# A graph layer and a mixture of experts in one kernel: experts' results wait in DRAM until the edges are done

## The chip, the cores and the metric

The kernel runs on one core of a Trainium2 chip. The metric is device time in microseconds (us) of one launch. Times below are either medians of several runs, or come from one profiled execution, whose trace all views of the profile answer from.

## The reference, cut to what matters

The input is 6250 nodes with 256 features, and 100,000 edges sorted by destination. A layer of graph attention comes first, then a mixture of 8 experts, of which each node uses two. In short form:

```python
xn  = layer_norm(layernorm(x)); h = xn @ W                 # 8 heads of 32
e   = leaky_relu(a_src[src] + a_dst[dst])                  # edges and self loops
agg = segment_softmax_sum(e, h[src], dst)                  # by destination node
o   = layer_norm(agg + xn @ W_res + bias)
x1  = x + o + gelu_tanh(o @ ffn_w1 + ffn_b1) @ ffn_w2 + ffn_b2
p   = softmax(layernorm(x1) @ Wr + br)                     # the two best of 8 experts
out = x1 + sum over the two experts e of
      weight_e * (gelu(ln_e(x1) @ W1[e] + b1[e]) @ W2[e] + b2[e])
```

So every row of `out` is written once (x1) and then has two experts' results added to it.

## The kernel before, in words

All arithmetic is in float32. A first stage (up to about 190 us) normalises the nodes, computes `h` and stores a table `tab_s` of its rows in DRAM.

**The edges.** The edges are handled in 196 steps of four tiles of 128 edges. In a step POOL issues four indirect DMAs that gather rows of `tab_s` by source node (`fetch`, L809), DVE weighs the rows (`weigh`, L847 to L851), and PE adds them up by destination with one-hot matrices (L866, L891). `gs`, the tile of gathered rows, has 4 buffers. The groups of edges run from the last destination to the first, so nodes at the end are finished first.

**Work beside the edges.** While the edges still run, finished nodes go through their own feed-forward network (`node_unit`), choose their experts, and are written to `out` by SP and, with POOL's scatters (`scatter`, L1345), into lists by expert in DRAM (`xs`). As soon as a list has 256 tokens for an expert, a block of experts' work can start (`block_unit`). There are 56 blocks (NB). A block loads 2 MB of weights (`load_weights`, L1388 to L1390) and its 256 tokens (`load_block`, L1396) with SP's queue, transposes the tokens (`turn`, L963 and L970), runs eight parts of the first product (`up`: PE L978, ACT L981 with Gelu) and the second product (`down`: PE L988, into the one PSUM tile `py`). Then, in this order:

- `note` (DVE, L1409 to L1413) copies the destination row numbers from the tokens' tile into the small tile `to` (3 buffers) and works out the weights;
- `finish` (DVE, L1418) adds the bias and moves `py` to `yb`, a tile of 2 x 256 columns with 2 buffers. It frees `py`;
- `weigh_block` (ACT, L1424) multiplies by the weights, 128 rows at a time;
- `give_back` (POOL, L1428) is an indirect DMA that adds 128 rows of `yb` to their rows of `out`. A block needs two. As all of them write `out`, each one waits until the one before has landed.

A buffer of `yb` becomes free when both additions of its block have landed.

**The order.** Nothing is reordered on the chip: each engine, and each queue of DMAs, runs its instructions in the order in which the program issues them. That order is made by a small planner in the kernel. Every operation beside the edges is a `task` with an engine and a cost in us. In each step `run_tasks` issues, oldest first, those tasks whose inputs were issued early enough, until the engine's `room` for this step is used up: `ROOM` while the edges run, `ROOM_AFTER` behind them (`s >= NG + LASTST`, with 196 and 6). One step stands for some 7.7 us of PE's time, and a block is worth about two steps:

```python
g0 = task(lambda: give_back(0, env), "POOL", 2.6, [wb_])
stored.append(task(lambda: give_back(1, env), "POOL", 2.6, [g0]))
```

`stored` holds the tasks after which a buffer of `yb` may be used again: `finish` names the second last of them as an input.

Of the kernel before, what the change touches and what calls it, by code (L numbers as in the profile page):

```python
# [36 lines left out]
F32 = mybir.dt.float32  # L40
I32 = mybir.dt.int32
U32 = mybir.dt.uint32
AF = mybir.ActivationFunctionType
ALU = mybir.AluOpType
# [4 lines left out]
P = 128  # L49
# [12 lines left out]
ROOM = {"PE": 7.5, "DVE": 7.6, "ACT": 5.0, "POOL": 2.6, "SP": 1e9}  # L62
EDGES = {"PE": 1.3, "DVE": 2.0}
BEHIND = {"PE": 0.5, "DVE": 1.4}
ROOM_AFTER = {"PE": 7.7, "DVE": 7.0, "ACT": 7.0, "POOL": 5.2, "SP": 1e9}

QUEUE = 40.0

# [148 lines left out]
def gnn_moe_kernel(  # L217
# [28 lines left out]
    nc = tc.nc  # L246
    N, D = x.shape
# [36 lines left out]
    NG = len(order)  # L284
# [8 lines left out]
    NB = (2 * N + E * (BT - 1)) // BT  # L293
# [10 lines left out]
    dp = ctx.enter_context(tc.tile_pool(name="dram", bufs=1, space=DRAM))  # L304
    rp = ctx.enter_context(tc.tile_pool(name="route", bufs=1))
    gnn = ctx.enter_context(ExitStack())
# [8 lines left out]
    xp_d = dp.tile([NP, D], F32, name="xp_d")  # L315
    xt_d = dp.tile([NT, P, KD * P], F32, name="xt_d")
    xs = dp.tile([E * CAP + BT, DX], F32, name="xs")

    tab_a = dp.tile([NP + P, H], F32, name="tab_a")
    tab_m = dp.tile([NP + P, H], F32, name="tab_m")  # L320
# [124 lines left out]
    with ExitStack() as actx:  # L445
# [40 lines left out]
        for i in range(2):  # L486
# [3 lines left out]
                                    axis=AX.X, op=ALU.add)  # L490
# [184 lines left out]
        for t0 in range(0, NT, G):  # L675
# [15 lines left out]
            for j in range(n):  # L691
# [37 lines left out]
                ap=[[4 * 2 * H, m1 - m0], [1, W32 * 2 * H]]))  # L729
# [3 lines left out]
            for a, k0, b0, b1 in ((acc_lo, 0, t0, min(t1, KHI + 2)),  # L733
                                  (acc_hi, KHI, max(t0, KHI + 2), t1)):
                if b0 < b1:
                    m, i = b1 - b0, slice(b0 - t0, b1 - t0)
                    a = a[:, b0 - k0:b1 - k0, :]
# [31 lines left out]
    cw = gnn.enter_context(tc.tile_pool(name="cw", bufs=2))  # L769
# [139 lines left out]
    LASTST = 6  # L909
# [16 lines left out]
    pending = []  # L926
    held = set()

    def task(*a, **k):
        t = Task(*a, **k)  # L930
        pending.append(t)
        return t

    def run_tasks(s, room):

        more = True
        while more:
            more = False
            for t in list(pending):
                if (t.take in held or room[t.eng] <= 0.0  # L940
                        or any(d.step is None or d.step + gap > s for d, gap in t.deps)):
                    continue
                pending.remove(t)
                t.step = s
                room[t.eng] -= t.cost
                if t.take:
                    held.add(t.take)
                if t.free:
                    held.remove(t.free)
                t.fn()  # L950
                more = True

    def back(tasks, n):

        return tasks[-n:][:1] if len(tasks) >= n else []
# [37 lines left out]
    def net(env, src, deps, w1, w2, func, b, more=(), scale=None):  # L993

        n = env["n"]
        tn = task(lambda: turn(src(), "in", env, scale and scale()), "PE", 0.3 * n,
                  [*deps, *[(d, 0) for d in back(ups_, 2)]])
        free = [(d, 0) for d in back(downs_, 2)]
        ups = [task(lambda c=c: up(c, env, w1(), func, b()), "PE", 0.46 * n, [tn, *more, *free])
               for c in range(KF)]  # L1000
        dn = []
        for j in range(n):
            for c in (0, KF // 2):
                dn.append(task(lambda j=j, c=c: down(j, c, c + KF // 2, env, w2()), "PE", 1.85,
                               [(dn[-1], 0)] if dn else [ups[-1]], take=None if dn else "py"))
        turns.append(tn)
        ups_.append(ups[-1])
        downs_.append(dn[-1])
        return dn[-1]
# [208 lines left out]
    ebf = rp.tile([P, NB], F32, name="ebf")  # L1218
    rowi = rp.tile([P, NB], I32, name="rowi")
    ebi = rp.tile([P, NB], I32, name="ebi")  # L1220
    endi = rp.tile([P, E], I32, name="endi")
    for t_, v_ in ((cnt, 0.0), (nfull, 0.0), (listed, 0.0), (rowf, float(E * CAP)), (ebf, 0.0)):
        nc.vector.memset(t_, v_)
# [115 lines left out]
    between = cp.tile([P, 1], F32, name="between")  # L1339
# [65 lines left out]
    def note(b, env):  # L1405

        x = env["xb"]
        to = cw.tile([P, 2], I32, name="to", bufs=3)
        nc.vector.tensor_copy(to, x.bitcast(I32)[:, :, D])  # L1409
        wt = cw.tile([P, 2], F32, name="wt", bufs=3)  # L1410
        nc.vector.scalar_tensor_tensor(wt, x[:, :, D + 1], ebf[:, b:b + 1], x[:, :, D + 3],
                                       op0=ALU.is_equal, op1=ALU.mult)
        nc.vector.tensor_add(wt, wt, x[:, :, D + 2])  # L1413
        env["to"], env["wt"] = to, wt

    def finish(env):
        yb = cw.tile([P, 2, D], F32, name="yb")
        nc.vector.tensor_tensor(yb, env["py"], env["w"][2][:, None, :].to_broadcast([P, 2, D]),  # L1418
                                op=ALU.add)
        env["yb"] = yb  # L1420
# [3 lines left out]
            nc.scalar.activation(env["yb"][:, j, :], env["yb"][:, j, :], AF.Copy,  # L1424
                                 scale=env["wt"][:, j:j + 1])

    def give_back(j, env):
        nc.gpsimd.indirect_dma_start(  # L1428
            out=out, out_offset=bass.IndirectOffsetOnAxis(ap=env["to"][:, j:j + 1], axis=0),
            in_=env["yb"][:, j, :], in_offset=None, compute_op=ALU.add, bounds_check=N - 1,  # L1430
            oob_is_err=False)

    def block_loads(b):
        env = {"n": 2}
# [8 lines left out]
    def block_unit(b, env):  # L1443
        no = task(lambda: note(b, env), "DVE", 0.6,
                  [(env["lx"], 2), *[(d, 0) for d in back(stored, 3)]])
        dn = net(env, lambda: env["xb"], [(env["lx"], 2), env["lp"]], lambda: env["w"][0],
                 lambda: env["w"][1], AF.Gelu, lambda: env["pc"][:, 0, :],
                 more=[(env["lw"], 2)], scale=lambda: env["pc"][:, 0, KF:])
        fi = task(lambda: finish(env), "DVE", 0.7, [dn, *[(d, 0) for d in back(stored, 2)]],
                  free="py")  # L1450
        wb_ = task(lambda: weigh_block(env), "ACT", 0.9, [fi, no])
        g0 = task(lambda: give_back(0, env), "POOL", 2.6, [wb_])
        stored.append(task(lambda: give_back(1, env), "POOL", 2.6, [g0]))
        blocks.append(fi)
        notes.append(no)


    units = [(t, 2) for t in range(NT - 2, 0, -2)]
    if NT % 2:
        units.append((0, 1))  # L1460
    units = [(t, n, order.index((first_group(t), groups[first_group(t)][1] - 1)))
             for t, n in units]
# [4 lines left out]
    notes = []  # L1467
    blocks, stored, cleared, sure, chunked, moew, last_hi, ahead = [], [], [], [], [0], [], [], []
    EARLY = 10
    s, u, since, was_nodes = 0, 0, [], False  # L1470

    with tc.manual_schedule():
        nc.sync.dma_start(xs[E * CAP:, :].rearrange("(p r) d -> p r d", r=2), blank[:, :2])
        while s < NG + LASTST or pending or u < len(units) or len(blocks) < NB:
            for g in range(s, min(s + EARLY, NG)):
                if order[g][0] // GC not in gds:
                    fetch_nodes(order[g][0] // GC)
            for f, d in STAGES:
                if 0 <= s - d < NG:
                    f(s - d)  # L1480
            if s == NG + LASTST:
                edges.close()
            if len(firsts) < len(units) and len(firsts) <= s + 1:
                first_unit(len(firsts))
            if len(firsts) == len(units) and firsts[-1].step is not None and fp:
                first_.close()
                fp = None
            if last_hi and last_hi[0].step is not None and not moew and not fp:
                hi_pool.close()
                moew.append(ctx.enter_context(tc.tile_pool(name="moew", bufs=2, side="right")))  # L1490
            nb = len(blocks) + len(ahead)
            if moew and len(ahead) < 2 and nb < NB and any(n > nb for n, _ in sure):
                block_loads(nb)

            while sum(t.cost for t in pending if t.eng == "PE") < QUEUE:
                if (u < len(units) and units[u][2] <= s - LASTST
                        and not (ahead and was_nodes)):
                    was_nodes = True
                    node_unit(u)
                    since.append(u)  # L1500
                    u += 1
                    if u % 2 == 0 or u == len(units):
                        chunk_tasks(since, u == len(units), u == len(units) - 1)
                        since = []
                elif ahead:
                    was_nodes = False
                    block_unit(*ahead.pop(0))
                else:
                    break
            room = dict(ROOM if s < NG + LASTST else ROOM_AFTER)  # L1510
            if s < NG + LASTST:
                g = s - 5
                ends = 0 <= g < NG and order[g][1] == groups[order[g][0]][1] - 1
                for e in EDGES:
                    room[e] -= EDGES[e] + ends * BEHIND[e]
            run_tasks(s, room)
            s += 1


# [29 lines left out]
```

## Time and profile before

| | us |
|---|---|
| median of 3 runs | 2020.89 (2017.11 to 2022.29) |
| the profiled execution: its own time | 2020.45 |
| its span, first to last instruction | 2018.6 |
| last gather of the edges issued (POOL L809) | about 1572 |
| `finish` of block 29 / 45 / 55 (DVE L1418, numbered from 0) | 1554.6 / 1854.1 / 2007.0 |

| engine | busy us | share of the span |
|---|---|---|
| PE, matmuls | 1682.6 | 83% |
| POOL | 1130.1 | 56% |
| DVE | 1081.7 | 54% |
| ACT | 724.4 | 36% |

The span consists of stages with different limits, so the shares of the whole say little: the stage before the edges ends at about 190 us, the edges with other work beside them last until about 1575 us, and after that only blocks of experts are left. [...] Between two such instructions stands a gap of 0.30 us that the profile calls "issue": POOL waits for nothing that can be seen, but it does nothing else either.

### The profile page before, as it was taken

To read this page: it belongs to the slowest core of one execution; us is meant where nothing else is said; L and a number is where in the kernel's file an instruction comes from. 1 tells how busy PE (TensorE), PEld (TensorE's weight loads), DVE (VectorE), ACT (ScalarE), POOL (GpSimd) and SP (SyncE) were. 2 spreads that over 40 slices of the span, in tenths; PEclk is the share of its full clock that TensorE was granted. 3 is DMA by queue.
4 is the path that set the end of the run, shared out by engine and by line. 5 is a ranking of instruction groups with operands and counts; after the bars stand their busy time and mean duration, and the time that the engine had idled before them with its cause. 6 is when DMAs were issued, how large, how long until landed. Compare 5 with 4: busy or idle time off the path is not lost. (4 is left out here: it accounts for less than half of the span.)

```text
span 2018.6 us, 28952 instructions
## 1 busy us (share of the span) xinstructions
PE 1682.6 (83%) x8737; PEld 1288.4 (64%) x8737; DVE 1081.7 (54%) x3978; ACT 724.4 (36%) x1626; POOL 1130.1 (56%) x1171
## 2 busy tenths in 40 slices
PE   4835897877877988989999997987999679999997
PEld 3523665555655766767667775765767467777776
DVE  8836878887788764756566663544535112100000
ACT  3821223323233443334344342333344134333332
POOL 2037755665656766576777787777777322112212
PEclk8978899888877999999999998998999889999999
DMA  4977664645436657465576647766767464666551
GB/s 131 278 216 220 187 187 135 185 134 164 124 112 198 188 133 216 128 184 171 154 216 197 193 131 229 212 183 180 242 200 207 156 178 118 201 183 186 163 181 48
DMA packets 251308, 355.73 MB, mean 176 GB/s; under 512 B 47521, under 2 KB 205633, under 8 KB 251148
## 3 DMA queue, kind: packets, MB, share of 16 engines
q1 hardware_dynamic: 187660, 211.04, 32.4%
q0 software_dynamic: 60176, 139.33, 26.9%
q10 hardware_dynamic: 3312, 3.48, 0.5%
q8 instruction: 70, 1.15, 0.2%
q14 instruction: 90, 0.74, 0.1%
HBM read 290.38 MB, written 68.44 MB: 178 GB/s over the span
## 5 line engine op out<-in xcount | busy, mean ns | idle before, releaser
L809 POOL DMA_INDIRECT gs<-tab_s,srce x784 | 812.1, 1036 | 364.2 <-issue 198.9
L978 PE MATMUL ph<-turned_in,w1b 128*128 128x256 f32 x1792 | 420.5, 389 | 53.3 <-ACT ht L981 38.0
L988 PE MATMUL py<-w2b,ht 128*128 128x256 f32 x1792 | 406.9, 386 | 11.1 <-DVE lg L1118 5.7
L978 PEld LDWEIGHTS ph<-turned_in,w1b 128*128 128x128 f32 x1792 | 320.2, 192 | 131.1 <-ACT ht L981 58.3
L988 PEld LDWEIGHTS py<-w2b,ht 128*128 128x128 f32 x1792 | 345.1, 194 | 61.8 <-DVE lg L1118 7.1
L1428 POOL DMA_INDIRECT out_dram<-yb,to x112 | 182.2, 1626 | 348.8 <-ACT yb L1424 141.1
L981 ACT ACTIVATE ht<-ph,pc 128x256 f32<-128x256 f32 x448 | 209.8, 473 | 214.6 <-PE ph L978 214.0
L1418 DVE TENSOR_TENSOR yb<-py,b2b 128x512 f32<-128x512 f32 x56 | 38.6, 690 | 389.5 <-PE py L988 319.6
L851 DVE TENSOR_TENSOR msg<-gs,msg 128x1024 f32<-128x1024 f32 x196 | 240.5, 1227 | 6.7
L988 PE MATMUL py<-w_sb,ht 128*128 128x256 f32 x784 | 190.8, 405 | 17.3 <-DVE lg L1118 15.0
L978 PE MATMUL ph<-turned_in,w_sb 128*128 128x256 f32 (+1 forms) x800 | 191.4, 392 | 14.2 <-ACT ht L981 14.2
L988 PEld LDWEIGHTS py<-w_sb,ht 128*128 128x128 f32 x784 | 158.8, 205 | 46.7 <-DVE lg L1118 19.5
L978 PEld LDWEIGHTS ph<-turned_in,w_sb 128*128 128x128 f32 x800 | 149.5, 199 | 44.6 <-ACT ht L981 20.1
L870 ACT ACTIVATE part<-pl 128x264 f32<-128x264 f32 x110 | 42.8, 389 | 326.7 <-PE pl L866 324.1
L833 ACT ACTIVATE oht<-pt 128x128 f32<-128x128 f32 x196 | 53.9, 275 | 273.2 <-PE pt L831 234.4
L866 PE MATMUL pl<-msg,oh 128*32 128x264 f32 x1568 | 131.1, 406 | 15.3 <-DVE msg L851 15.1
L1345 POOL DMA_INDIRECT xs<-xe,slot x98 | 103.6, 1057 | 57.1 <-DMA xs<-blank 22.4
L981 ACT ACTIVATE ht<-ph,prm 128x256 f32<-128x256 f32 (+1 forms) x200 | 92.3, 469 | 113.3 <-PE ph L978 113.0
L891 PE MATMUL p<-part,oh 128*128 128x264 f32 x220 | 84.3, 469 | 56.3 <-DVE acc_hi L902 37.3
L831 PEld LDWEIGHTS pt<-ident,oh 128*128 128x128 f32 x196 | 27.5, 140 | 138.4 <-issue 81.3
L970 ACT ACTIVATE turned_in<-pt,pc 128x256 f32<-128x256 f32 x112 | 57.0, 559 | 154.8 <-PE pt L963 144.5
L831 PE MATMUL pt<-ident,oh 128*128 128x128 f32 x196 | 65.4, 334 | 49.5 <-ACT turned_in L970 22.9
(324 smaller groups left out, 1912.2 us busy)
## 6 DMA issues: line engine op xcount, KB each, us to landing
w1b<-in_L_ffn_W_dram SPq DMA_DIRECT2D x56, 1024.0 KB
w2b<-in_L_ffn_W_dram SPq DMA_DIRECT2D x56, 1024.0 KB
xb<-xs SPq DMA_DIRECT2D x56, 260.0 KB
gs<-tab_s,srce POOLq DMA_INDIRECT x784
b2b<-in_L_ffn_b_dram SPq DMA_DIRECT2D x56, 128.0 KB
tab_s<-hg SPq DMA_DIRECT2D x12, 544.0 KB
xg<-in_x_dram SPq DMA_DIRECT2D x12, 512.0 KB
xt_d<-xt SPq DMA_DIRECT2D x12, 512.0 KB
```

Source lines behind the costliest of these rows:

```text
L809: nc.gpsimd.indirect_dma_start(out=gs[:, j, :], out_offset=None, in_=tab_s, in_offset=bass.IndirectOffsetOnAxis(ap=srce[:, t:t + 1], axis=0))
L831: nc.tensor.transpose(po[:, 0, :P], live[s, "oh"].rearrange("p j r -> p (j r)"), ident)
L833: nc.scalar.activation(oht, po[:, 0, :P], AF.Copy)
L851: nc.vector.tensor_tensor(msg[:, :, :D].rearrange("p t (h d) -> p t h d", h=H), gs[:, :, :D].rearrange("p t (h d) -> p t h d", h=H), msg[: ...
L866: nc.tensor.matmul(pl[j * W32:(j + 1) * W32, :], oh[:, j, :], msg[:, j, :], start=i == 0, stop=last)
L891: nc.tensor.matmul(p2, oh2, part, start=True, stop=True)
L970: nc.scalar.activation(xt[:, k, :n * P], pt[:, k, :n * P], AF.Identity, bias=scale[:, KD + k:KD + k + 1], scale=scale[:, k:k + 1])
L978: nc.tensor.matmul(ph[:, :W], w1[:, k, c * P:(c + 1) * P], env["in"][:, k, :W], start=k == 0, stop=k == KD - 1)
L981: nc.scalar.activation(ht[:, :W], ph[:, :W], func, bias=b[:, c:c + 1], scale=1.0)
L988: nc.tensor.matmul(env["py"][:, j, :], env["ht", c][:, j * P:(j + 1) * P], w2[:, c, :], start=c == 0, stop=c == KF - 1)
L1345: st = nc.gpsimd.indirect_dma_start(out=xs, out_offset=bass.IndirectOffsetOnAxis(ap=slots[k][:n, t:t + 1], axis=0), in_=xes[u // 2][:n, pl ...
L1428: nc.gpsimd.indirect_dma_start(out=out, out_offset=bass.IndirectOffsetOnAxis(ap=env["to"][:, j:j + 1], axis=0), in_=env["yb"][:, j, :], in ...
```

## The change

A block whose `block_unit` is planned before step NG - 4 no longer adds its result to `out` at once. SP stores its `yb` to a DRAM tensor `ys` (`put_by`). When the last step of the edges is over, a pool `back` with 3 buffers is opened; from then on SP loads stored blocks again (`load_back`), at most one a step and with at most two waiting, and POOL adds them to `out`, at most one a step, and only if POOL's room for the step is not used up. Blocks that are planned later add their results from `yb` as before.

The two additions of one block are issued directly one after the other, and are declared free of each other (a token is in an expert's list once); a small memset stands between them. Additions of different blocks keep their order. The task of a block has a cost of 4.4, and `ROOM_AFTER` for POOL goes from 5.2 to 6.0. The row numbers move from the small tile `to` with 3 buffers to `tos`, which has a place for every block.

```diff
-ROOM_AFTER = {"PE": 7.7, "DVE": 7.0, "ACT": 7.0, "POOL": 5.2, "SP": 1e9}
+ROOM_AFTER = {"PE": 7.7, "DVE": 7.0, "ACT": 7.0, "POOL": 6.0, "SP": 1e9}
...
+    ys = dp.tile([NB, P, 2 * D], F32, name="ys")
...
+    tos = rp.tile([P, NB, 2], I32, name="tos")
...
-        to = cw.tile([P, 2], I32, name="to", bufs=3)
-        nc.vector.tensor_copy(to, x.bitcast(I32)[:, :, D])
+        nc.vector.tensor_copy(tos[:, b], x.bitcast(I32)[:, :, D])
...
-    def give_back(j, env):
-        nc.gpsimd.indirect_dma_start(
-            out=out, out_offset=bass.IndirectOffsetOnAxis(ap=env["to"][:, j:j + 1], axis=0),
-            in_=env["yb"][:, j, :], in_offset=None, compute_op=ALU.add, bounds_check=N - 1,
-            oob_is_err=False)
+    def give_back(b, yb):
+        for j in range(2):
+            st = nc.gpsimd.indirect_dma_start(
+                out=out, out_offset=bass.IndirectOffsetOnAxis(ap=tos[:, b, j:j + 1], axis=0),
+                in_=yb[:, j, :], in_offset=None, compute_op=ALU.add, bounds_check=N - 1,
+                oob_is_err=False)
+            tc.add_to_no_dep_group(f"block{b}", st.ins)
+            tc.declare_no_dep(st.ins, group=f"block{b}",
+                              reason="an expert has a token once, and what is no token nowhere")
+            nc.gpsimd.memset(between, 0.0)
+
+    def put_by(b, env):
+        nc.sync.dma_start(ys[b].rearrange("p (j d) -> p j d", j=2), env["yb"])
+
+    def load_back(b):
+        yb = backp[0].tile([P, 2, D], F32, name="back")
+        nc.sync.dma_start(yb, ys[b].rearrange("p (j d) -> p j d", j=2))
+        return yb
...
-        g0 = task(lambda: give_back(0, env), "POOL", 2.6, [wb_])
-        stored.append(task(lambda: give_back(1, env), "POOL", 2.6, [g0]))
+        if s < NG - 4:
+            stored.append(task(lambda: put_by(b, env), "SP", 0.0, [wb_]))
+            put.append((b, stored[-1]))
+        else:
+            stored.append(task(lambda: give_back(b, env["yb"]), "POOL", 4.4, [wb_]))
...
             if s == NG + LASTST:
                 edges.close()
+                backp.append(gnn.enter_context(tc.tile_pool(name="back", bufs=3)))
...
             run_tasks(s, room)
+
+            if backs and backs[0][2] < s and room["POOL"] > 0:
+                give_back(*backs.pop(0)[:2])
+            if backp and put and put[0][1].step is not None and len(backs) < 2:
+                b = put.pop(0)[0]
+                backs.append((b, load_back(b), s))
             s += 1
```

More of the change, by code (lines that the diff above doesn't have):

```diff
@@ L1413, in note @@
         nc.vector.tensor_add(wt, wt, x[:, :, D + 2])
-        env["to"], env["wt"] = to, wt
+        env["wt"] = wt
     def finish(env):
@@ L1469, in gnn_moe_kernel @@
     EARLY = 10
+    put, backs, backp = [], [], []
     s, u, since, was_nodes = 0, 0, [], False
@@ L1473, in gnn_moe_kernel @@
         nc.sync.dma_start(xs[E * CAP:, :].rearrange("(p r) d -> p r d", r=2), blank[:, :2])
-        while s < NG + LASTST or pending or u < len(units) or len(blocks) < NB:
+        while s < NG + LASTST or pending or u < len(units) or len(blocks) < NB or put or backs:
             for g in range(s, min(s + EARLY, NG)):
```

## The prediction

> **What bounds the kernel now.** I first read the page's rows of slices: PE is at 9 of 10 for most of the last three quarters, but POOL is at 7 just where PE dips. So I asked for the busy time of each engine by stage (columns: stretch, length, then busy us and count for PE, PEld, DVE, ACT, POOL, then clock, DMA share, GB/s):
>
> ```profile
> 640.00:1000.00 360.00, 324.68 (x1761) 248.31 (x1761) 227.83 (x839) 147.61 (x310) 252.00 (x266) 0.96 0.57 167
> 1000.00:1575.00 575.00, 516.80 (x2930) 396.32 (x2929) 312.87 (x1057) 219.85 (x481) 447.65 (x424) 0.97 0.67 196
> 1740.00:2007.00 267.00, 255.77 (x1189) 210.48 (x1188) 21.19 (x81) 95.66 (x205) 55.44 (x36) 1.00 0.55 161
> ```
>
> Then POOL's groups in the second half of the edges, 1000 to 1575 us:
>
> ```profile
> L809 POOL DMA_INDIRECT gs<-tab_s,srce x332 | 347.4, 1046 | 100.7 <-issue 89.2 <-DVE msg L850 2.1 <-DMA gs<-tab_s,srce 1.8
> L1428 POOL DMA_INDIRECT out_dram<-yb,to x41 | 69.0, 1682 | 19.7 <-issue 8.4 <-DMA out_dram<-yb,to 5.3 <-DMA out_dram<-xin 2.0
> L1345 POOL DMA_INDIRECT xs<-xe,slot x26 | 28.6, 1099 | 7.1 <-issue 5.3 <-DMA xb<-xs 1.0 <-DVE acc_lo L902 0.3
> L1351 POOL MEMSET between<- 128x1 f32 x25 | 3.0, 118 | 0.0
> ```
>
> Busy plus idle is 448.1 + 88.7 + 35.7 + 3.0 = 575.5 us in 575: the idle is the 0.3 us between instructions, so POOL is full there and sets the pace, and the 41 additions are 88.7 us of it. PE has 516.8 us of work in the same stretch. From 640 to 1000 POOL isn't full. From 1740 on PE sets the pace: a block takes 15.28 us (`finish` of block 54 to that of 55: 1991.7 to 2007.0), in which POOL makes two additions and otherwise waits. How they follow each other is in POOL's timeline (start, length, idle before and what ended it):
>
> ```profile
> 1665.97 1.55 POOL L1428 DMA_INDIRECT out_dram<-yb,to  x1 [9.30 <-ACT yb L1424]
> 1670.44 1.55 POOL L1428 DMA_INDIRECT out_dram<-yb,to  x1 [2.91 <-DMA out_dram<-yb,to]
> ...
> 1953.02 1.55 POOL L1428 DMA_INDIRECT out_dram<-yb,to  x1 [6.20 <-ACT ht L981]
> 1959.97 1.55 POOL L1428 DMA_INDIRECT out_dram<-yb,to  x1 [5.41 <-DMA out_dram<-yb,to]
> ```
>
> The second addition of a block starts when the first has landed: 4.47 us after its start in quiet, 6.95 us beside weights. POOL itself works 1.55 us of that; the rest is the transfer.
>
> **What the Trainium skill says.** Perfetto Trace Analysis, "Identifying the Most-Contended Engine": for GpSimd, occupancy is a fair measure of how near the limit it is; here it has to be read with the issue gaps, 447.65 of 575 busy and yet full. DMA: Bandwidth & Descriptors, "Issuing engines are not separate DMA queues": DMAs from all engines run on the same 16 DMA engines and interleave. The trace agrees: the same addition takes 4.47 or 6.95 us. The same page, "Rules for kernel authors": an accumulating DMA must wait for the semaphore of an earlier access to the same bytes. So two blocks, which may share a token, have to wait for each other; the trace shows that wait as L1428 <- DMA out_dram.
>
> **The change part by part.** PE's, ACT's and DVE's instructions keep their number and order (the built order of both kernels, set side by side). Only POOL's and SP's queues change.
>
> (a) Beside the edges, 29 blocks' 58 additions leave POOL. In 1000 to 1575 its demand falls from 575.5 to 575.5 - 88.7 = 486.8 us, below PE's 516.8. PE is late next. It can't be busy all the time: it was 95.8% in the tail (255.77 of 267), where nothing held it; 516.8 / 0.958 = 539.5, a gain of 35.5 us. Bounds: at the 90.2% of the stretch 640 to 1000, where POOL was not full, 573, a gain of 2; at 100%, 58. Before 1000 I add 4.5 us: DVE's waits for `to` and `yb`, which end with additions, are gone (63.2 and 25.3 us in 640 to 1575, mostly within the stretch already counted). Sum: **40 us earlier**, between 5 and 60.
>
> (b) 32 stores and 32 loads of 256 KB come onto SP's queue, 16.8 MB to 355.7. An issue there takes 0.38 us, as for `w1b`. A store waits for ACT L1424; behind it stand loads of nodes and weights of blocks one to two ahead. A block comes every 30 us in the edges (`finish` of blocks 0 to 29: 684.0 to 1554.6, 29 intervals), and `yb` now waits for a store where it waited for two additions. I take 0, hidden by that slack. DVE's copy of the row numbers stays the same 0.16 us and loses only its wait. If the cover fails, the next `w1b` is late by the wait, at most 2 us or so in each of 32 blocks (64 us); the gain from freeing `yb` earlier could be as much as the 25.3 us above. A load waits for additions three places before it; it is needed about two pairs later, so also 0.
>
> (c) Behind the edges POOL now has 56 pairs where it had 27 blocks' additions. Its built order there, with B for a stored block and Y for one straight from `yb`: BBB Y BB Y BBBB Y BB Y BB (one token scatter) BB Y BB Y BBB Y BB Y BBB Y BB Y BBB Y BB Y, then 12 Y. Up to the twelfth Y, which is block 43, these are 32 + 12 = 44 pairs. A pair waits for both landings of the pair before (the built waits say so). Its second instruction comes 1.55 + 0.12 (memset) + 0.19 (the gap after L1351) = 1.86 us after the first. From there I take what an addition took from start to the next start when the next waited only for it: the 23 such intervals in the tail, without the last three blocks, have a mean of 5.75 us, between 4.46 and 8.96. No row shows a pair. Lower bound: 1.86 + 4.46 = 6.3 (quiet). Upper: 1.86 + 6.95 = 8.8 (always beside weights). As a slower tail has the weights' traffic less dense, I take 5.64, so **7.5 us a pair**.
>
> The start: the token scatters before the first pair end at 1609.8 in the trace; 40 us earlier is 1569.8. The pairs end at 1569.8 + 44 x 7.5 + 2.5 (two token scatters at 1.25) = 1902.3. Now the wait that matters: `finish` of block 45 needs the `yb` of block 43, so it can't be before 1902.3; it was at 1854.1. Until then `py` stays full, and behind it PE's `down` of block 46 waits; its `up` is already done. After it comes 7.1 us of L988, 0.7 of DVE and gaps, 8.3 us to `finish` of block 46, then 9 x 15.28 = 137.5 for the rest: 1902.3 + 8.3 + 137.5 = 2048.1. POOL catches up there, since one pair a block is 7.5 in 15.28.
>
> (d) Behind the last `finish` were 2018.6 - 2007.0 = 11.6 us, with two additions one after the other at 3.46 us apart. Side by side they are 1.86 apart: 1.6 saved, 10.0 left.
>
> Sum of spans: 2048.1 + 10.0 = 2058.1, against 2018.6. The execution's own time is 1.85 us over its span and 0.44 below the median, so **2060 us**, +2.0%. The ACT stall at 1615 (DVE waited 44.7 us for `yb` at 1624.65) goes as well, 11.5 us of PE, but counts nothing when POOL's chain sets the end.
>
> **The rivals.** They differ in the price of a pair and in the gain beside the edges.
>
> - *Pairs are cheap, the end is faster.* With everything else as above the change breaks even at 7.5 - 39.5 / 44 = 6.6 us a pair. For it: 8 of the 23 intervals are under 5 us (6.9 with 1.86), and a pair may suffer one burst of weights once, not twice. Against: even in quiet a pair has 6.3. At 6.3 and a gain of 55 beside the edges the time is 2060 - 53 - 15 = 1992. If a pair took 5.3 or less, PE would set the pace throughout: 2020.5 - 40 - 11.5 - 1.6 = 1967; no interval seen allows that. Together 0.16.
> - *No gain beside the edges.* POOL's fullness would be a mirror of PE's pace: 5 us instead of 40, 2095. Against: PE is idle 58 us in that stretch while POOL has no gap. 0.07.
> - *The halves are not side by side.* A pair would be 2 x 5.75 = 11.5, and the time 2060 + 44 x 4 = 2236. The built waits of the second half name only its own semaphore's earlier use and ACT, so 0.01.
> - *POOL's chain as worked out*, slower by 2030 to 2090: 0.71. What lies between the first rival and this, no change that can be told: 0.05. About 0.3% (6 us) is what a measurement of this kernel can tell from no change.
>
> **How the numbers follow.** Slower: 0.71 + 0.07 + 0.01 = 0.79; same 0.05; faster 0.16. The likeliest case alone runs from 2030 (6.8 us a pair) to 2090 (8.2). For the range I reach down to 2004, which leaves some 0.1 of the cheap pairs out, and up to 2095, which takes in the second rival.
>
> **What would show it.** In the profile after: from 1000 us on, PE busy 95% or more until the last gather, which comes at about 1532; POOL with gaps over 0.3 us there. Behind it L1431 in pairs 1.9 us apart, pair after pair at about 7.5 us with "DMA out_dram" as releaser, for some 330 us; DVE L1420 waiting on DMA out_dram for many us in each of blocks 34 to 45; PE idle a quarter of the time until about 1900, then 15.28 us a block. It would be wrong if pairs come at 6.5 us or less, if PE stays at 95% through the tail, or if the last gather is not earlier.

## The result, and the profile after

| | before | after |
|---|---|---|
| median, us (4 runs each, side by side) | 2021.59 (2017.11 to 2024.95) | 2084.01 (2082.66 to 2090.01) |
| ratio, 95% interval | | 1.0316 [1.0287, 1.0345] |
| span of the profiled execution, us | 2018.6 | 2080.3 |
| last gather issued, us | 1571.2 | 1524.8 |
| from there to the end, us | 447.4 | 555.5 |

The change makes the kernel 3.2% slower. The edges end 46.4 us earlier, and the tail, as the stretch from the last gather to the end is called here, is 108.1 us longer; the difference is the 61.7 us between the spans. (The last gather is the start of the last `L811` in POOL's timeline. `L811` and the other lines of the kernel after stand two to three lines further down than in the kernel before.) Beside three of the experiments below (e9, e10, e11) the kernel before itself took 2204.95 us, for a reason that isn't known, so these three are compared by their ratio to it and by the length of their tails.

The busy times by stage, of the kernel after (stretch, length, then busy us and count of PE, PEld, DVE, ACT, POOL, then clock, DMA share, GB/s):

```profile
640.00:1000.00 360.00, 322.90 (x1772) 247.01 (x1771) 229.81 (x856) 149.13 (x312) 230.08 (x253) 0.97 0.56 171
1000.00:1540.00 540.00, 507.73 (x2912) 390.29 (x2911) 307.05 (x1033) 217.43 (x474) 369.38 (x376) 1.00 0.65 208
1740.00:1900.00 160.00, 111.69 (x436) 89.21 (x436) 8.12 (x30) 35.41 (x76) 70.44 (x84) 0.82 0.70 173
```

In the second half of the edges PE is now busy 94% (507.73 of 540). In 1740 to 1900, in the tail, it was busy 95.9% (153.45 of 160, the line is shown in the last section) and is 70% (111.69 of 160). The busy share flatters it: it makes 436 matmuls there and not 716, at a granted clock of 0.82 and not 1.00. POOL's groups of the kernel after, 1000 to 1540 us, show that POOL is no longer what sets the pace of the edges:

```profile
L811 POOL DMA_INDIRECT gs<-tab_s,srce x324 | 338.0, 1043 | 153.7 <-issue 83.3 <-DVE oh L820 46.9 <-DVE msg L853 17.0
```

Of the 153.7 us of idle time ahead of the gathers, only 83.3 are the fixed gaps of 0.30 us between two indirect DMAs; in 63.9 (46.9 and 17.0) POOL waits for DVE. DVE's `weigh` is the only reader of the gathered rows, so POOL waits for one of their buffers to come free. The additions have gone from this stage and POOL has slack.

POOL's timeline of the kernel after shows the pairs, the two additions of a block, in the tail (start, length, idle before and what ended it):

```profile
1844.07 1.56 POOL L1431 DMA_INDIRECT out_dram<-back,tos  x1 [2.28 <-DMA out_dram<-back,tos]
1845.93 1.57 POOL L1431 DMA_INDIRECT out_dram<-back,tos  x1 [0.19 <-issue]
1850.60 1.56 POOL L1431 DMA_INDIRECT out_dram<-yb,tos  x1 [2.98 <-ACT turned_in L972]
1852.46 1.57 POOL L1431 DMA_INDIRECT out_dram<-yb,tos  x1 [0.19 <-issue]
1860.81 1.56 POOL L1431 DMA_INDIRECT out_dram<-back,tos  x1 [6.67 <-issue]
1867.18 1.56 POOL L1431 DMA_INDIRECT out_dram<-back,tos  x1 [2.83 <-issue]
```

The halves of a pair stand 1.86 us apart. From pair to pair it is 6.53, then 10.21, then 6.37 us. The names after the arrows are not to be trusted here: an addition waits for several semaphores, and ACT had long been done; what ends the wait is the landing of the pair before.

What waits in the tail, 1550 to 1990 us of the kernel after (engine, line and what it waited for: us in total, times, longest). PE first, then DVE, then SP's queue:

```profile
PE ph L980 <- DMA w1b<-in_L_ffn_W_dram: 54.4, 9, 15.0
PE pt L965 <- DMA xb<-xs: 33.9, 4, 23.8
PE ph L980 <- ACT ht L983: 20.1, 6, 13.3
...
DVE yb L1420 <- DMA out_dram<-yb,tos: 172.6, 9, 22.9
...
SPq L1445 <- DMA out_dram<-back,tos: 190.4, 28, 13.7
```

DVE's `finish` stands for 172.6 us until additions have landed: the wait that was predicted. But PE's largest waits are for weights and for tokens, and SP, which fetches both, stands for 190.4 us at `load_back` until a buffer `back` is added and free. That second wait was not in the prediction.

### The profile page after: what moved, and what is told of

It is laid out like the page before. It is cut to its first block, busy times and chain, and to the rows that moved or that the text cites. A ratio compares the mean times of both kernels' runs of the same rounds, so it can differ in the third digit from the quotient of the medians.

```text
span 2080.3 us, 29100 instructions
## 1 busy us (share of the span) xinstructions
PE 1694.9 (81%) x8737; PEld 1295.2 (62%) x8737; DVE 1080.5 (52%) x3978; ACT 725.4 (35%) x1626; POOL 1131.8 (54%) x1283
## 5 line engine op out<-in xcount | busy, mean ns | idle before, releaser
L811 POOL DMA_INDIRECT gs<-tab_s,srce x784 | 807.5, 1030 | 455.1 <-issue 195.6
L980 PE MATMUL ph<-turned_in,w1b 128*128 128x256 f32 x1792 | 435.9, 399 | 93.2 <-DMA w1b<-in_L_ffn_W_dram 54.4
L980 PEld LDWEIGHTS ph<-turned_in,w1b 128*128 128x128 f32 x1792 | 331.5, 198 | 175.3 <-issue 56.7
L990 PE MATMUL py<-w2b,ht 128*128 128x256 f32 x1792 | 402.5, 383 | 14.8 <-DVE yb L1420 5.7
L1431 POOL DMA_INDIRECT out_dram<-yb,tos x48 | 75.0, 1562 | 183.7 <-ACT yb L1426 112.3
L1431 POOL DMA_INDIRECT out_dram<-back,tos x64 | 100.0, 1563 | 136.4 <-issue 82.4
```

What stands on the lines that cost most here:

```text
L811: nc.gpsimd.indirect_dma_start(out=gs[:, j, :], out_offset=None, in_=tab_s, in_offset=bass.IndirectOffsetOnAxis(ap=srce[:, t:t + 1], axis=0))
L980: nc.tensor.matmul(ph[:, :W], w1[:, k, c * P:(c + 1) * P], env["in"][:, k, :W], start=k == 0, stop=k == KD - 1)
L990: nc.tensor.matmul(env["py"][:, j, :], env["ht", c][:, j * P:(j + 1) * P], w2[:, c, :], start=c == 0, stop=c == KF - 1)
L1431: st = nc.gpsimd.indirect_dma_start(out=out, out_offset=bass.IndirectOffsetOnAxis(ap=tos[:, b, j:j + 1], axis=0), in_=yb[:, j, :], in_offs ...
```

## The experiments

**No additions of stored blocks.** The first two kernels leave out the additions of the 32 stored blocks, one of them their loads as well. They tell what the returns cost, and whether the loads or the additions cost it.

```diff
e1:  -            if backs and ...: give_back(...)   # and the load_back below it
e2:  -                give_back(*backs.pop(0)[:2])
     +                backs.pop(0)
```

> The changed kernel without the way back: the 32 stored blocks are never loaded and never added to the output (left out). Theory (the chain of pairs behind the edges sets the end): with 24 pairs left, PE sets the pace again at 15.28 us a block. Block 33 is finished at 1596.5 in the changed kernel against 1655.6 before, 59 us earlier, and the last additions save 1.6: 2020.5 - 61 = 1960 us, within 10. Rival (what is slow behind the edges is PE's own work, at a lower clock, or weights that come late for a reason of their own): it stays above 2040.

> The changed kernel with the stored blocks loaded again, but never added (their additions are left out). Theory (the chain of additions): as without the way back at all, 1960 to 1970 us, since the loads are 8.4 MB spread over 200 us. Rival (the loads' traffic, or their places on SP's queue, make the weights late): 2040 us or more, as the loads are all there.

Measured: 1965.41 us, ratio 0.9715 [0.9687, 0.9743], and 1967.11 us, ratio 0.9734 [0.9706, 0.9763], both as expected. The traffic of 32 loads and their places in SP's queue cost nothing that can be told, as long as no load has to wait for an addition. The tail is 435.4 us without returns and 433.6 with loads alone, against 555.5: the 64 additions, and what waits for them, make it about 120 us longer.

**Halves one after another.** The declaration that frees the halves of a block of each other is taken out.

```diff
-            tc.add_to_no_dep_group(f"block{b}", st.ins)
-            tc.declare_no_dep(st.ins, group=f"block{b}", ...)
```

> The changed kernel with the two additions of a block one after the other again. Theory: a pair takes 2 x 5.75 = 11.5 us in place of 7.56, and 44 pairs lie on the path: 2084 + 44 x 3.94 = 2257 us (2230 to 2280). Rival (the chain of additions is not on the path, weights are): within 20 us of 2084.

Measured: 2191.78 us, ratio 1.0836 [1.0806, 1.0867]. The direction is right, the size was too large: from the first pair (1591.0) to the last stored one, 42 pairs later (2009.6), a pair takes 9.97 us and not 11.5. Its POOL timeline shows why:

```profile
1856.98 1.56 POOL L1431 DMA_INDIRECT out_dram<-back,tos  x1 [2.42 <-DMA out_dram<-yb,tos]
1860.99 1.57 POOL L1431 DMA_INDIRECT out_dram<-back,tos  x1 [2.34 <-DMA out_dram<-back,tos]
1865.10 1.56 POOL L1431 DMA_INDIRECT out_dram<-back,tos  x1 [2.43 <-DMA out_dram<-back,tos]
```

Here one addition follows another at 4.0 to 4.1 us, and over the 42 pairs at 4.98 on average (9.97 / 2); the 5.75 of the kernel before was too high for this tail. That a slower tail has fewer weights on the way in the same time would explain it, but isn't shown by itself. Still, the tail is 661.8 us long and not 555.5: side by side is worth 106 us of it.

**Which buffer holds PE?** Two rival answers: the two buffers of `yb` (DVE's wait), or the three of `back` (SP's wait). Each gets eight buffers alone, then both together.

```diff
e5:  +        latep.append(... tile_pool(name="late", bufs=8))   # yb behind the edges
e6:  -        backp.append(... tile_pool(name="back", bufs=3))
     +        backp.append(... tile_pool(name="back", bufs=8))
e9:  both
```

> The changed kernel with 8 buffers for stored blocks that were loaded, in place of 3, so that SP's queue doesn't wait for additions before it issues the next weights. In the changed kernel SP waited 190 us at these loads, and PE 51 us for w1b and 30 us for tokens behind the edges. Theory (the chain of pairs sets the end and these waits lie beside it): 2075 to 2085 us; PE's wait turns into a wait for yb. Rival (SP's blocked queue and late weights are the cause): 2000 to 2035 us.

> The changed kernel, but behind the edges yb has 8 buffers of its own in place of 2, so finish of a block waits for the pair eight blocks back. Theory (PE is held by yb, and yb by the chain of pairs): PE runs ahead of POOL, and the end is then POOL's whole chain, 56 pairs from 1584.5 on at 7.5 to 7.8 us: 2005 to 2021, and some 5 us after it: 2012 to 2030 us. Rival (weights late behind SP's waits): 2060 us or more.

Measured: 2095.56 us with eight `back`, ratio 1.0369 [1.0336, 1.0402], no gain, and 10 us above the range; 2068.46 us with eight `yb`, 1.0234 [1.0209, 1.026], a gain, but far from the 2012 to 2030 expected. Eight `back` (1550 to 1990 us) clear SP's wait for additions at `load_back`, of which 0.4 us are left, and DVE's grows:

```profile
DVE yb L1420 <- DMA out_dram<-yb,tos: 191.5, 8, 29.0
```

Eight `yb`, the same stretch, clear DVE's wait, and SP still stands as long as before. PE's largest waits, then SP's queue:

```profile
PE ph L980 <- DMA w1b<-in_L_ffn_W_dram: 57.7, 9, 14.3
PE pt L965 <- DMA xb<-xs: 36.3, 4, 23.3
...
SPq L1445 <- DMA out_dram<-back,tos: 189.2, 29, 13.9
```

So PE seems to be tied to POOL's chain twice, at about the same pace: through DVE and `yb`, and through SP and `back`. Cutting one leaves the other. Then both were cut:

> The changed kernel with both buffers widened behind the edges: yb 8 in place of 2, and loaded blocks 8 in place of 3. With yb alone (2068 us) PE waited 87 us for w1b and tokens, whose loads stood on SP's queue behind loads that waited for additions; with loaded blocks alone (2096) DVE waited 191 us for yb. Theory (two links tie PE to the chain of pairs, and either one is enough): with both cut PE runs at its own pace, and the end is POOL's whole chain, 56 pairs of 7.6 to 7.8 us from 1587 on, and 5 us: 2018 to 2032 us. Rival (the two together don't free PE, as what makes weights late is traffic): 2050 us or more.

Measured: 2228.12 us, ratio 1.0093 [1.0066, 1.0119]. As a ratio the expected range is about 0.998 to 1.005, so it was missed. But in this run and in e10 and e11 the stages ahead of the tail were slower: their last gathers are at 1716 to 1746 us, where the runs above have 1525 to 1532. In the tail a block takes PE 15.28 us in them too, so it is the tails that can be compared. The tail of e9 is 494.1 us, against 555.5 (after), 565.8 (e6) and 533.8 (e5): only with both does PE come near its own pace. Behind edges that end at 1524.8, as in the kernel after, such a tail would end at about 2019 us, inside the range; this is an estimate, no run shows it. The busy times over 160 us of the tail of e9, then SP's wait in 1740 to 2180 us:

```profile
1940.00:2100.00 160.00, 146.15 (x671) 119.94 (x670) 12.37 (x50) 54.30 (x117) 70.43 (x84) 0.97 0.80 207
...
SPq L1445 <- DMA out_dram<-back,tos: 46.6, 9, 13.8
```

POOL makes as many pairs as in the kernel after (70.43 us and 84 instructions, there 70.44 and 84), at 207 GB/s and not 173, and PE is busy 146 us where it was 112 (671 matmuls and not 436; the kernel before has 716). So what the additions take from PE is for the most part not their traffic, but the two in-order waits, and SP's is shorter here, not gone. The rest of e9's extra tail is POOL's chain itself: from the first pair (1776.0) to the end (2209.6) are 56 pairs in 433.6 us, 7.74 each, without a pause of note. From this follows an estimate of the room for pairs: without returns there are 357 us from the first pair to the last `finish` (e1: 1595.8 to 1953.0), room for some 47 pairs at 7.6, and the change wants 56.

**Fewer stored blocks.** 22 blocks are stored, from the eleventh on, and at most one is added back for a block: 46 pairs. The edges lose little: the last gather is at 1530.1 (e7) and 1525.7 (e8), against 1524.8 in the kernel after.

```diff
-        if s < NG - 4:
+        if s < NG - 4 and b >= 10:
...
-            if backs and backs[0][2] < s and room["POOL"] > 0:
+            if backs and backs[0][2] < s and room["POOL"] > 5:
```

> The changed kernel with only the blocks from the 11th on stored (22; the first ten are added at once, where POOL was not full), and at most one of them added back for each block behind the edges (only in a step without a block's own pair). Theory: POOL stays below PE beside the edges, so nearly all of the 46 us there stay; behind them 2 pairs a block are 15.1 us against PE's 15.3, so PE is held only where pairs meet weights: 1975 to 2005 us, faster than the kernel before. Rival (stored results cost by their traffic or SP's places, not by pairs per block): 2040 us or more.

> The same with 8 buffers of yb behind the edges. Theory: pairs that meet weights are evened out over 8 blocks, so PE is hardly held: 1965 to 1985 us, 10 to 20 us under the same kernel with 2 buffers. Rival (the rest over 1960 is late weights): no difference between the two.

Measured: 2017.3 us, ratio 0.9974 [0.9964, 0.9983], and with eight `yb` 2002.19 us, 0.9904 [0.9873, 0.9935]. The step between the two is as expected; both miss their range, by 12 and 17 us. What the two expectations left out is SP's tie, which is still there in both. In e8, 1550 to 1990 us, SP's queue shows:

```profile
SPq L1445 <- DMA out_dram<-back,tos: 145.3, 19, 14.2
```

> 22 stored blocks, at most one added back for each block behind the edges, and both buffers 8. Theory (what the kernel with 22 blocks and 8 buffers of yb, 2002 us, has over the 1965 without any way back is SP's queue held by loads): 1968 to 1985 us. Rival (it is the traffic of loads and additions on the DMA engines that delays weights): within 8 us of 2002.

> Only every other block from the 12th on is stored (11 blocks), one added back for each block behind the edges, both buffers 8. In 1000 to 1575 POOL then has 575 - 22 x 2.16 + 19 x 0.3 = 533 us of work, just below what PE needs (517 / 0.95 = 544). Theory: most of the gain beside the edges stays, 30 of 46 us, and behind them 35 pairs hold nobody: 1970 to 1985 us. Rival (POOL has to be well below PE before PE gains): 1990 us or more.

Measured: ratio 0.9932 [0.9902, 0.9962] with eight of both, and 1.0021 [0.9994, 1.0049] with only every second of these blocks stored. As ratios the expected ranges are about 0.974 to 0.982 and 0.975 to 0.982, so both were missed, and both lie where their rivals have them: the traffic of loads and additions delays weights (e10), and POOL has to be well below PE before PE gains (e11). Their tails are 458.0 and 454.4 us; storing fewer shortens the tail by little once the pairs fit. The profiled executions, 2203.6 and 2200.3 us long, don't show where e10's better median comes from. So neither rival is excluded here, and e11's stays open. The same kernel as e10 was run once more:

> The same kernel as e10_fewer_88 (22 blocks stored from the eleventh on, at most one added back per block, eight buffers for `yb` behind the edges and eight for `back`), run again, because the runs beside e10 had every stage ahead of the tail some 9% slower than in all runs before them. Two ties: where the kernel before takes about 2020, the last gather is at about 1530 and the tail behind it about 455 to 460 long, as in e10, so 1985 to 1992 in all, a ratio of 0.98 to 0.986. Rival, that eight `back` buffers only let more loads and additions stand beside the weights, as in e6_back8: no better than e8_fewer_yb8, a ratio of 0.99 or above. Where the kernel before again takes about 2200: a ratio of 0.99 to 0.996 as in e10, and nothing is told apart.

Measured: 1989.42 us (1982.56 to 1992.02), ratio 0.9829 [0.9805, 0.9852], as the two ties have it (4 us above the range that e10 was given); the rival, 0.99 or above, is excluded. This is the best of all complete kernels here. In 160 us of its tail POOL makes the same 21 pairs as in the kernel after, and PE, at a granted clock of 1.00, doesn't lose anything to them:

```profile
1740.00:1900.00 160.00, 153.45 (x715) 126.44 (x714) 12.41 (x50) 57.65 (x124) 70.34 (x84) 1.00 0.78 207
```

The tails set side by side: with 56 pairs 555.5 us, and 494.1 with both ties cut (e9); with 46 pairs, at most one stored block for each block, 488.9 (e7), and 456.3 with both ties cut (e12). So the ties are worth 61 or 33 us, the fewer pairs 67 or 38, and neither replaces the other.

**Side by side alone.** Nothing is stored; the halves of a block are freed of each other. The smaller parts of the change stay: `tos`, one task for both halves, and POOL's room of 6.0.

```diff
-        if s < NG - 4:
+        if False:
```

> The other half of the change alone: both additions of a block side by side, nothing stored, every block adds its result at once, as before the change. Theory: beside the edges POOL's time for an addition is what costs, 1.68 us and a gap, and it is still there (plus 0.3 us for each memset), so no gain there; at the end 1.6 us are saved and the stall of 11.5 us at 1615 may shrink: 2010 to 2022 us. Rival (the wait for landing was what held POOL and DVE beside the edges): 1995 us or less.

Measured: 2003.96 us (1998.22 to 2013.05), ratio 0.9901 [0.9873, 0.9929]: more than expected, and not the 1995 or less of its rival. The execution with the profile was the slowest of the four, 7.4 us below the profiled one of before; in it the last gather is at 1571.2 as before, and the waits of DVE and PE in the tail are smaller (1550 to 1990 us):

```profile
DVE yb L1420 <- DMA out_dram<-yb,tos: 9.8, 1, 9.8
PE ph L980 <- ACT ht L983: 7.6, 4, 3.5
```

In the kernel before:

```profile
DVE yb L1418 <- DMA out_dram<-yb,to: 44.7, 1, 44.7
PE ph L978 <- ACT ht L981: 15.5, 4, 11.5
```

How much of this comes from the halves and how much from the smaller parts is not told apart, and what gives the other executions their further 8 to 15 us stays open. Set beside e12, each against the kernel before, it tells what storing with the ties cut adds: 0.9829 against 0.9901, some 0.7%. The rest of e12's gain is there without storing anything.

## Why the prediction came out as it did, point by point

The forecast, slower at 2060 us, had the right sign and in the main the right mechanism: POOL's chain of pairs holds PE through `yb`. It was 24 us too low. Two terms were too small: the loads ahead of the first pair, put at 0, and the step from the end of the chain back to PE. The second tie, through SP and `back`, was not in it.

- **(a) The gain beside the edges**: 46.4 us earlier, 40 forecast. Gather 460 starts at 1003.1 instead of 1013.2, so 10.1 come before about 1000 us, where 4.5 were allowed, and 36.3 behind it, where 35.5 were. PE reached 94.0% and not 95.8%, though, and so the 95% that were to show it were missed by a little. The second rival (no gain) is out.
- **(c) The price of a pair**: 7.5 forecast. The first pair starts at 1584.51, the 45th at 1916.96: 332.45 / 44 = 7.56. But the mean hides two sizes. Of the 44 intervals, 14 have the issue of a `w1b` or `w2b` between 3 us ahead of the pair and 4 us after its start; their mean is 9.83 (7.5 to 11.4). The other 30 have 6.49 (5.8 to 9.4). Both bounds were off: 8.8 was too low for a pair that meets weights, and 6.3 too high for one in quiet, since the three additions of the last blocks in the kernel before, 3.44 to 3.46 us after the one ahead of them, had been left out (so "no interval seen allows that", of pairs at 5.3, didn't hold). The first rival's condition, 6.6 us or less, is what pairs cost without weights; with 2 MB of weights for each block it wasn't the mean. That 7.5 met 7.56 was in part luck: it was 1.86 us plus 5.64 for one addition, but with the 4.98 of e3's tail the same sum gives 6.84. One addition was taken as too dear, and the second beside it as free but for its later start. The halves that are not side by side take 9.97 (e3), where that rival had 11.5.
- **The start of the chain**, forecast 1569.8, was 1584.5. This is the term that failed most, by 14.7 us. The loads had been put down as 0, since a load "is needed about two pairs later". Ahead of the first load there is no pair. SP's and POOL's timelines of the kernel after:

```profile
1561.60 0.98 SPq L1441 DMA_DIRECT2D ys<-yb  x1
1570.38 0.38 SPq L1399 DMA_DIRECT2D xb<-xs  x1
1571.55 0.38 SPq L1391 DMA_DIRECT2D w1b<-in_L_ffn_W_dram  x1
1572.18 0.37 SPq L1392 DMA_DIRECT2D w2b<-in_L_ffn_W_dram  x1
...
1575.49 0.80 SPq L1445 DMA_DIRECT2D back<-ys  x2
```

```profile
1564.57 0.11 POOL L1354 MEMSET between<- 128x1 f32 x1
1584.51 1.62 POOL L1431 DMA_INDIRECT out_dram<-back,tos  x1 [19.83 <-DVE rsv L437]
```

POOL's token scatters are over at 1564.7, five us ahead of the forecast. SP, in order, holds its next token load until they have landed (1570.38), then issues 2 MB of weights, and the first load of a stored block only at 1575.49. From 1571.5 to 1584.5 the DMA engines are busy 91%, so it shares them with the weights. POOL idles 19.83 us; this is what stood as 0. The profile names a DVE instruction as the releaser. By its order the pair waits for the load, as it needs `back`; how the 9 us from issue to pair divide is not shown.

- **From the chain to PE.** `finish` of block 45 was at 1916.4, forecast 1902.3; the start explains that. Then the forecast gave 8.3 us to the next `finish`, because the `up` of block 46 would be done. It was 16.1. ACT, PE and DVE in the timelines of the kernel after:

```profile
1902.53 1.02 ACT L972 ACTIVATE turned_in<-pt,pc 128x256 f32<-128x256 f32 x2 [8.40 <-PE pt L965]
1917.14 0.91 ACT L1426 ACTIVATE yb<-yb,wt 128x256 f32<-128x256 f32 x2 [13.59 <-DVE yb L1420]
1917.96 0.82 ACT L983 ACTIVATE ht<-ph,pc 128x256 f32<-128x256 f32 x2
...
1903.15 2.02 PE L980 MATMUL ph<-turned_in,w1b 128*128 128x256 f32 x8 [0.66 <-ACT turned_in L972]
1918.46 6.84 PE L980 MATMUL ph<-turned_in,w1b 128*128 128x256 f32 x23 [13.30 <-ACT ht L983]
...
1916.37 0.69 DVE L1420 TENSOR_TENSOR yb<-py,b2b 128x512 f32<-128x512 f32 x1 [22.91 <-DMA out_dram<-yb,tos]
...
1932.46 0.69 DVE L1420 TENSOR_TENSOR yb<-py,b2b 128x512 f32<-128x512 f32 x1 [14.26 <-PE py L990]
```

`weigh_block` of block 45 waits for `finish` (1916.37) and stands in ACT's queue ahead of the Gelus of block 46. Two parts of the first product fill `ph`, and PE waits 13.3 us for ACT. So the wait on `yb` stops not only `py` but ACT, and through ACT the `up` too: 7.8 us more than the sum had. With the 14.1 by which `finish` of block 45 was late that is 21.9, of the 22.2 by which the span was missed (2080.3 against 2058.1).

- **(b) Loads and stores.** The stores' waits are there, SP's queue in 640 to 1540 us of the kernel after:

```profile
SPq L1441 <- ACT yb L1426: 150.2, 21, 10.2
```

They are longer than the 2 us or so that had been put as the most, 7.2 us on average and up to 10.2. No loss follows from them that can be seen, with PE at 94%: the slack seems to cover them, as forecast. The loads' traffic costs nothing either (e2). But "needed about two pairs later, so also 0" was wrong in kind: a load waits for additions, and behind it on SP stand weights and tokens. In this kernel it moves the end little, since `yb` holds PE at the same pace (e6); it is why e5 brought so little, as e9 shows.
- **(d) Behind the last `finish`**: forecast 10.0, measured 2080.3 - 2070.1 = 10.2. (The 15.28 us of a block are right for the tail, but not the difference of the two `finish` named for it: the last one comes 15.34 us after the one before.)

On the skill's places. Its occupancy rule for GpSimd (Perfetto Trace Analysis, "Identifying the Most-Contended Engine") again has to be read with the waits: POOL's busy share in 1740 to 1900 is 44%, and its chain of landings sets the pace of the tail. That DMAs from all engines interleave on 16 DMA engines (DMA: Bandwidth & Descriptors, "Issuing engines are not separate DMA queues") agrees with the 6.49 us of a pair without weights and the 9.83 of one beside them.

## What to carry to other kernels

Work that is moved off a full engine has to fit where it goes: count the slots before (here room for some 47 pairs, an estimate, and 56 came), and store only as many as fit. A chain that runs late costs others mainly through what waits for it in order, so look for every tie, on SP and ACT too, and cut them together: eight buffers on one side gained 0.8% or nothing, and on both sides, with the count that fits, the slower change became 1.7% faster than the kernel before. Test the small part of a change by itself: 1.0% of it came without moving any work. And the first item of a moved queue has nobody ahead to hide its load.

## What had not been expected of the hardware

Adding to `out` ran beside the matmuls of e12 at no cost to PE: 21 pairs in 160 us, at 207 GB/s in all, leave PE at 153.45 us busy, the same as the kernel before, whose line of this stretch (columns as above) has half the work on POOL:

```profile
1740.00:1900.00 160.00, 153.45 (x716) 126.62 (x716) 12.78 (x51) 56.47 (x121) 33.78 (x22) 1.00 0.62 179
```

And two additions side by side cost less than two in a chain, though more than one: 6.49 us for a pair without weights, against 4.0 to 4.1 for each of two in a chain.

What a burst of weights does to an addition can be seen in the DMA packets of the kernel before. In quiet, behind 1980 us, the first packet of an addition comes 2.12 us after its start. Where a `w1b` or `w2b` is issued 0.1 to 0.9 us after the start (14 cases), it comes after 4.3 to 5.7. So much of the delay lies ahead of the first packet.
